# Rows of x1 stored behind the last packed load, x1's turns one chunk ahead and in both halves, first pieces of x0T and Wk at the head of a queue each

## The chip, the cores and the metric

The kernel runs on one core of one Trainium2 chip. The metric is the device time in microseconds (us) of one execution. TensorE (PE) multiplies, VectorE (DVE) and ScalarE (ACT) work on rows of elements, GpSimd (POOL) does the same more slowly, and SyncE (SP) mostly issues DMA transfers. Each engine takes its instructions in the order of the program, and the engines wait for each other by semaphores.

## The reference, cut to what matters

Four layers follow each other on x with 2 x 1024 rows of 512; each one adds its result to its input and normalizes the row.

```
x = layernorm(x + linear_attention(x))       # k = elu(x Wk)+1, q = elu(x Wq)+1, v = x Wv
x = layernorm(x + fp4_swiglu(x))             # weights: 4-bit codes with a scale per group of 128
x = layernorm(x + gated_linear_attention(x)) # 16 chunks of 64 rows per batch
x = layernorm(x + expert_choice_ffn(x))      # the 512 best rows of each batch
```

The second layer is `y = (silu(x Wg) * (x Wu)) Wd` with 1408 inner features, then y over its root mean square. The change touches the first layer's start, the unpacking of the 4-bit weights, and the way the first layer's result x1 gets into the second layer.

## The kernel before

The rows are worked on in four blocks of 512 (`blk` 0 to 3, two per batch).

**First layer, from 0 to about 243 us.** The schedule of this part is made by a scheduler: it keeps an order by priority, readiness and its own estimate of times; `tc.issue_after(x)` and the helper `behind()` (which is `issue_after` of the last PE instruction) hold instructions back behind another. The loads at the top are in pieces so that PE can start early: `part_of_Wk` (L166, on SP) and `part_of_x` (L169, on ACT or SP). Before them PE runs seven products of ones, `idle` (L358). Block 0's k is made by plain products `kp` (L637): for each k of four contraction pieces, four row tiles, with k = 0 cut in two halves of 256 columns. Later projections use `by_seven` (L390), seven products in place of eight, with copies from PE's bank such as L411 and L417. `layernorm` of blocks 0 to 2 is done in `o_products`: statistics on DVE (L226, L227), a power and four normalizing passes on POOL (L221).

**Unpacking.** `unpack` (L281) loads a packed weight piece `pk` (L285, on SP, two buffers), shifts and masks it on DVE (L288, L289) and converts it on ACT (L292). 27 such pieces are spread by `unpack_some` over the first layer. SP issues its DMAs in order, so what stands behind a waiting DMA waits too.

**How x1 gets turned.** Block 0 is transposed on PE. For blocks 1 to 3 the normalized rows are stored to DRAM by `put_rows` (L246) and read back by `get_squares` (L255) in 32 x 32 squares into a tile `x1S`; then `turn_x1` (L1086, DVE) transposes inside the squares a quarter at a time, `high_part` (L1091, ACT) rounds the quarter to a high part and `low_part` (L1095, DVE) subtracts to get the low part. `turn_x1` of a quarter comes before its two parts.

**Second layer, from about 243 to 490 us.** This loop is in an order written out by hand (`manual_schedule`), for PE, ACT, DVE and POOL. A chunk is 128 of the 1408 inner features for one block: 11 chunks a block, n from 0 to 43. In each half of step n:

```python
old.step(0, 2 + half, ACT)      # gate of chunk n-1, contraction piece 2 or 3
new.step(0, half, ACT)          # gate of chunk n, piece 0 or 1
old.step(1, 2 + half, DVE)      # up of chunk n-1
new.step(1, half, ACT)          # up of chunk n
y_pair(m, part)                 # two row tiles of the down product of an earlier chunk
for job in later.get((n, half), ()):
    job()
```

`step` is a product on PE (`in_two`, L950, high and low part), followed by a scaling of the bank in place by ACT (L975) or DVE (L977); the last piece of a gate gives the silu on ACT (L979), the last piece of an up gives `whole` on DVE (L981), which POOL splits (L983, L984). The next piece is added into the scaled bank, so PE needs each scaling. `y_pair` multiplies each down product by a ratio on DVE (L1009). The jobs in `later`, filled by `add(n, half, job)`, are appended to the end of a half: the turns and parts of x1, the statistics (L226) and the scaling (L1023) of the block before, stores and loads, turns of x2.

Of the kernel before, what the change touches and what calls it, by code (L numbers as in the profile page):

```python
# [24 lines left out]
KC = C // P  # L25
I_FF = 1408
NI = I_FF // P
# [46 lines left out]
def body(ctx: ExitStack, tc: tile.TileContext, a: dict, out: bass.AP):  # L74
    nc = tc.nc
# [12 lines left out]
    def bank(ring, name):  # L88
        i = rings[ring][turn_of[ring] % len(rings[ring])]
        turn_of[ring] += 1  # L90
        return psum.tile([P, 512], F32, tag=f"bank{i}", name=name)
# [15 lines left out]
    def wgu_at(k, at, n):  # L107

        i = sum(at >= to for to in gu_parts[1:])
        return wgu[i][:, k, at - gu_parts[i] : at - gu_parts[i] + n]  # L110
# [35 lines left out]
    def xT_slot(i, name, dtype=F32):  # L146
        return xtp.tile([P, KC, 512], dtype, tag=f"xT{i}", name=name)

    def new_xT(blk):
        t = xT_slot(blk % 2, f"x0T{blk}")  # L150
        return t, a["xT"][:, blk * 512 : (blk + 1) * 512].rearrange("(k p) t -> p k t", p=P)
# [12 lines left out]
    t, src = new_xT(0)  # L164

    def part_of_Wk(k, at, to):  # L166
        nc.sync.dma_start(out=Wk[:, k, at:to], in_=a["WkT"][k * P : (k + 1) * P, at:to])

    def part_of_x(by, k, at, to):  # L169
        by.dma_start(out=t[:, k, at:to], in_=src[:, k, at:to])  # L170

    part_of_Wk(0, 0, 256)
    part_of_x(nc.scalar, 0, 0, 128)
    part_of_x(nc.sync, 0, 128, 512)
    for k in range(1, KC):
        part_of_x(nc.scalar, k, 0, 512)
    part_of_Wk(0, 256, 512)
    for k in range(1, KC):
        part_of_Wk(k, 0, 512)
    xT = {0: t}  # L180
# [60 lines left out]
    def put_rows(blk, name, part=range(4)):  # L241

        if (blk, name) not in rows_of:
            rows_of[blk, name] = dram.tile([512, C], F32, name=f"{name}{blk}")
        at, to = part[0], part[-1] + 1
        nc.sync.dma_start(  # L246
            out=rows_of[blk, name][P * at : P * to].rearrange("(c p) d -> p c d", p=P), in_=x_t[blk][:, at:to]
        )

    def get_squares(blk, name, room, part=range(4)):  # L250

        at, to = part[0], part[-1] + 1
        src = rows_of[blk, name][P * at : P * to].rearrange("(tr j) (k g i) -> g j k tr i", j=32, k=KC, g=4)
        for g in range(4):
            nc.sync.dma_start(out=room[32 * g : 32 * g + 32].rearrange("j k (tr i) -> j k tr i", i=32), in_=src[g])  # L255
# [25 lines left out]
    def unpack(parts_, packed, n):  # L281

        pk = dq.tile([P, 704], I32, tag="pk", name="pk")[:, :n]
        src = bass.AP(packed.tensor, packed.offset, [packed.ap[0], (0, 8), packed.ap[1]])
        nc.sync.dma_start(out=pk, in_=src)  # L285


        nc.vector.tensor_scalar(pk, pk, shift, 3, ALU.logical_shift_left, ALU.arith_shift_right)  # L288
        nc.vector.tensor_scalar(pk, pk, CODE, None, ALU.bitwise_and)  # L289
        half = pk.bitcast(F16).rearrange("p (n two) -> p n two", two=2)[:, :, 1]  # L290
        for dst, cut in parts_:
            nc.scalar.activation(dst, half[:, cut], AF.Copy, scale=UNIT)  # L292

    def unpacking():
        n = 704
        for at in range(0, 2 * I_FF, n):
            borders = [at, *(x for x in gu_parts if at < x < at + n), at + n]
            for g in range(KC):
                yield [
                    (wgu_at(g, i, j - i), slice(i - at, j - at)) for i, j in zip(borders, borders[1:])  # L300
                ], a["gu"][16 * g : 16 * (g + 1), at : at + n], n
        for g in (*range(3, NI), *range(3)):
            yield [(wdn_group(g), slice(0, C))], a["dn"][16 * g : 16 * (g + 1), :], C

    to_unpack = unpacking()
    last_elu = [None]
    anchor = [None]

# [45 lines left out]
    nc.vector.memset(ones, 1.0)  # L354

    idle = bank("acc", "idle")
    for _ in range(7):
        ins = nc.tensor.matmul(idle[:, :P], ones, ones, start=True, stop=True).ins  # L358
    last_pe = [ins]

    def behind():

        return ExitStack() if last_pe[0] is None else tc.issue_after(last_pe[0])
# [188 lines left out]
    def o_products(blk):  # L552

        A11, A12, A21, A22 = (qT[blk][:, 2 * e : 2 * e + 2, 256 * t : 256 * t + 256] for t in range(2) for e in range(2))
        G = G_of[blk // 2]
        B11, _, B21, B22 = (G[:, 2 * e : 2 * e + 2, 256 * o : 256 * o + 256] for e in range(2) for o in range(2))
        T1, T2, T3, T4 = TG[blk // 2]

        def product(ps, a, b, first, t, o):

            with behind():
                for r in range(2):
                    for k in range(2):
                        ins = nc.tensor.matmul(
                            ps[:, 256 * r : 256 * r + 256], a[:, k, r * P : (r + 1) * P], b[:, k],
                            start=first and r == 0 and k == 0, stop=k == 1, skip_group_check=True,
                        ).ins
            last_pe[0] = ins
            x = x_t[blk][:, 2 * t : 2 * t + 2, 256 * o : 256 * o + 256]
            return nc.vector.tensor_add(x, x, ps.rearrange("p (r c) -> p r c", r=2)).ins  # L570

        if blk not in S_of:
            q_sums(blk)
        S1, S2 = S_of[blk]
        grow = acc_bank("grow")
        added = product(grow, A11, B11, True, 0, 0)
        with tc.issue_after(added):
            for rest in TG_rest:
                rest()
            TG_rest.clear()  # L580
            nc.vector.tensor_sub(A21, A11, A21)
        yield
        product(acc_bank("P2"), A12, B21, True, 0, 0)
        yield
        product(grow, S2, T2, False, 1, 0)
        nc.vector.tensor_sub(A12, A12, S2)
        yield
        side = acc_bank("P7")
        product(side, A21, T3, True, 1, 1)
        yield  # L590
        product(grow, S1, T1, False, 1, 1)
        yield
        product(side, A22, T4, False, 1, 0)
        yield
        product(grow, A12, B22, False, 0, 1)
        yield
        mv = mv_of[blk] = sp.tile([P, 4, 2], F32, tag="mv", name="mv")
        with tc.issue_after(weighed[0]):
            for i in range(4):
                row_stats(mv[:, i], x_t[blk][:, i])  # L600
            layernorm(x_t[blk], mv, by=nc.gpsimd)
        if blk:
            put_rows(blk, "x1r")
        yield

    def add_o(blk, i):
# [23 lines left out]
    pairs_of["k", 0] = [new_pair(f"k{t}") for t in range(2)]  # L630
    rings["mm"] = (4, 5, 1, 3)
    first = [mm_bank("kp") for _ in range(4)]
    with behind():
        for k in range(KC):
            for i in range(4):
                for o in (slice(0, 256), slice(256, 512)) if k == 0 else (slice(0, 512),):
                    ins = nc.tensor.matmul(  # L637
                        first[i][:, o], xT[0][:, k, tile_of(i)], Wk[:, k, o],
                        start=k == 0 and o.start == 0, stop=k == KC - 1, skip_group_check=True,
                    ).ins  # L640
    last_pe[0] = ins
    rings.update(mm=(0, 1), sum=(2, 3))
    turn_of.update(mm=0)
    Ts = {"k": sums_of_weights(Wk, slices(Tk, 0, 3))}
# [48 lines left out]
    for b in range(B):  # L693
        i, j = 2 * b, 2 * b + 1
# [42 lines left out]
        more()  # L737
    late = mv_of[3]
    unpack_some(1000)
    squares = {1: xT_slot(0, "x1S")}  # L740
    get_squares(1, "x1r", squares[1])
    sg = wk.tile([KC * FG, P], F32, name="sg", bufs=1)
    nc.gpsimd.tensor_copy(sg, gus)
    pg = mm_bank("pg")
# [186 lines left out]
    with tc.tile_pool(name="s2", bufs=1) as wk2:  # L931
# [144 lines left out]
        def add(n, half, job):  # L1076
            later.setdefault((n, half), []).append(job)
# [6 lines left out]
        def turn_x1(blk, i):  # L1084
            x1T[blk, i] = square_tile("x1T")
            nc.vector.transpose(x1T[blk, i], squares[blk][:, :, tile_of(i)])  # L1086

        def high_part(blk, i):
            if i == 0:
                parts_of[blk] = split_tiles(blk)  # L1090
            nc.scalar.copy(parts_of[blk][0][:, :, tile_of(i)], x1T[blk, i])  # L1091

        def low_part(blk, i):
            hi, lo = (t[:, :, tile_of(i)] for t in parts_of[blk])
            nc.vector.tensor_sub(lo, x1T[blk, i], hi.bitcast(F32))  # L1095
# [12 lines left out]
            nc.vector.transpose(xT[blk][:, :, tile_of(i)], squares[blk, i])  # L1108

        for blk in range(1, NB):  # L1110
            first = 5 if blk == 1 else NI * blk - 5
            for i in range(4):
                add(first + i, 1, lambda blk=blk, i=i: turn_x1(blk, i))
                add(first + i + 1, 0, lambda blk=blk, i=i: high_part(blk, i))
                add(first + i + 1, 1, lambda blk=blk, i=i: low_part(blk, i))
        add(8, 0, lambda: put_rows(3, "x1r"))
        add(NI + 1, 0, lambda: get_x1(2))
        add(2 * NI + 1, 0, lambda: get_x1(3))
        for blk in range(2):
            first = (23, 34)[blk]  # L1120
# [833 lines left out]
    _, xs = fetch(0)  # L1954
# [88 lines left out]
```

## Time and profile before

| | |
|---|---|
| median of 3 runs | 912.48 us (911.91 to 913.32) |
| profiled execution, its own time | 912.31 us |
| its span, first to last instruction | 910.5 us |
| busy: PE, DVE, ACT, POOL | 98%, 76%, 42%, 29% of the span |
| mean granted clock of PE | 0.997 |
| DMA | 60.66 MB, mean 67 GB/s |

The span is what the views below divide; the time of the execution is 1.8 us longer. PE's busy time says where PE had a product in flight, not that it ran at its best pace, so the waits and the pace of its products are read beside it. A number in square brackets in the timeline is the engine's idle time before an instruction and what ended it. An engine name with a q (SPq) is the queue that issues DMAs.

### The profile page before, as it was taken

What the parts mean: (1) busy time and instruction counts of PE and PEld (TensorE: products, weight loads), DVE (VectorE), ACT (ScalarE), POOL (GpSimd) and SP (SyncE); (2) the same over time, 40 slices, a digit from 0 to 9 for tenths busy, and PEclk for the clock granted to TensorE, in tenths of its full rate; (3) what the DMA queues carried; (4) which work ended last, traced back from release to release, by engine and by line L of the source; (5) the groups of instructions that cost most, each with busy time, mean ns of one, the idle gap of its engine ahead of it and who ended that gap; (6) DMA issues with size and microseconds to landing.
All of it is one profiled execution on the core that took longest, in us unless ns stands there. A gap on an engine that the chain in (4) does not pass through costs nothing.

```text
span 910.5 us, 10938 instructions
## 1 busy us (share of the span) xinstructions
PE 888.3 (98%) x3955; PEld 692.6 (76%) x3955; DVE 693.7 (76%) x1324; ACT 378.6 (42%) x644; POOL 263.4 (29%) x229
## 2 busy tenths in 40 slices
PE   8999999999999999999999999999999999999996
PEld 5667885688577887877877677788676888888886
DVE  2558994588879789798879875857977886898535
ACT  1345341454467786876867534131201223120000
POOL 0120074200474357457564302020250030000112
PEclk9999999999999999999999999999999999999999
DMA  9532222200441402604201500000024220230001
GB/s 328 195 112 67 74 75 81 68 14 1 86 135 46 47 1 56 84 1 114 72 0 47 208 1 1 1 1 1 0 93 139 94 85 9 99 133 1 13 35 47
DMA packets 70391, 60.66 MB, mean 67 GB/s; under 512 B 46622, under 2 KB 47178, under 8 KB 69825
## 3 DMA queue, kind: packets, MB, share of 16 engines
q1 hardware_dynamic: 67841, 54.89, 20.7%
q0 software_dynamic: 1920, 4.22, 1.2%
q10 hardware_dynamic: 576, 0.85, 0.3%
q8 instruction: 31, 0.51, 0.2%
q14 instruction: 23, 0.19, 0.1%
HBM read 46.27 MB, written 15.78 MB: 68 GB/s over the span
## 4 chain that ended last, share of the span: by engine, by line
PE 78%; DVE 13%; POOL 3%; issue 2%; ACT 2%; DMA 1%; POOLq 0%; SPq 0%; DVEq 0%; ACTq 0%
PE yp L1726 10%; PE hp L1640 9%; PE yp L950 8%; PE upp L950 8%; PE gatep L950 8%; PE go L918 7%; PE xk L441 5%; PE grow L390 4%; PE P L390 3%; PE kp L637 2%; PE ao L611 2%; PE ao L1513 2%; PE grow L1479 1%; DVE cmp L1564 1%; PE op L1351 1%
## 5 line engine op out<-in xcount | busy, mean ns | idle before, releaser
L1009 DVE TENSOR_TENSOR yp<-yp,ratio 128x512 f32<-128x512 f32 x160 | 103.2, 691 | 10.3 <-PE yp L950 9.9
L219 POOL TENSOR_TENSOR rs<-rs,table 128x4 f32<-128x4 f32 (+1 forms) x19 | 17.2, 904 | 293.9 <-DVE rs L218 293.7
L975 ACT ACTIVATE gatep<-gatep,scale 128x512 f32<-128x512 f32 x132 | 83.8, 656 | 40.0 <-PE gatep L950 37.2
L950 PE MATMUL gatep<-x1Tl,wgu 128*128 128x512 f32 x176 | 69.5, 395 | 3.5 <-DVE x1Tl L1095 3.2
L950 PE MATMUL upp<-x1Th,wgu 128*128 128x512 f32 x176 | 69.8, 396 | 0.7 <-DVE upp L977 0.7
L950 PE MATMUL gatep<-x1Th,wgu 128*128 128x512 f32 x176 | 70.3, 399 | 0.0
L950 PE MATMUL yp<-wdn,hlo 128*128 128x512 f32 x176 | 69.9, 397 | 0.2 <-POOL hlo L984 0.2
L950 PE MATMUL yp<-wdn,hhi 128*128 128x512 f32 x176 | 69.9, 397 | 0.0
L950 PE MATMUL upp<-x1Tl,wgu 128*128 128x512 f32 x176 | 68.9, 391 | 0.0
L975 ACT ACTIVATE upp<-upp,scale 128x512 f32<-128x512 f32 x88 | 57.8, 662 | 9.6 <-PE upp L950 3.6
L984 POOL TENSOR_TENSOR hlo<-whole,hhi 128x512 fp32r<-128x512 f32 x43 | 56.2, 1306 | 3.5
L983 POOL CAST hhi<-whole 128x512 fp32r<-128x512 f32 x43 | 26.3, 611 | 91.7 <-DVE whole L981 90.6
L981 DVE SCALAR_TENSOR_TENSOR whole<-upp,scale,silu 128x512 f32<-128x512 f32 x43 | 32.1, 747 | 19.7 <-PE upp L950 13.3
L918 PE MATMUL go<-spare,spare 128*128 128x256 f32 x192 | 44.0, 381 | 0.0
L441 PE MATMUL xk<-pair,x 128*128 128x512 f32 x96 | 42.7, 592 | 0.0
L226 DVE BATCH_NORM_STATS2 st<-x 128x6 f32<-128x512 f32 x64 | 42.3, 675 | 0.4
L950 PEld LDWEIGHTS gatep<-x1Tl,wgu 128*128 128x128 f32 x176 | 33.1, 188 | 12.1 <-DVE x1Tl L1095 4.1
L950 PEld LDWEIGHTS upp<-x1Th,wgu 128*128 128x128 f32 x176 | 33.0, 188 | 10.0 <-DVE upp L977 2.8
L1373 POOL TENSOR_TENSOR sum<-sum,sq 128x512 f32<-128x512 f32 x12 | 18.2, 1520 | 77.1 <-issue 67.5
L918 PEld LDWEIGHTS go<-spare,spare 128*128 128x128 f32 x192 | 36.0, 190 | 5.8 <-issue 1.2
L950 PEld LDWEIGHTS yp<-wdn,hhi 128*128 128x128 f32 x176 | 33.0, 188 | 9.5 <-DVE yp L1009 1.1
L950 PEld LDWEIGHTS gatep<-x1Th,wgu 128*128 128x128 f32 x176 | 33.1, 188 | 9.0 <-ACT gatep L975 1.1
(472 smaller groups left out, 2108.9 us busy)
## 6 DMA issues: line engine op xcount, KB each, us to landing
pk<-in_gu SPq DMA_DIRECT2D x16, 352.0 KB, 3.7
x<-in_x SPq DMA_DIRECT2D x4, 1024.0 KB, 15.3
w<-in_w SPq DMA_DIRECT2D x1, 4096.0 KB, 13.5
xs<-picked SPq DMA_DIRECT2D x4, 1024.0 KB, 5.1
out<-x SPq DMA_DIRECT2D x4, 1024.0 KB, 4.7
w<-in_w SPq DMA_DIRECT2D x4, 1024.0 KB, 5.5
x0T<-in_xT SPq DMA_DIRECT2D x3, 1024.0 KB, 6.9
x1r<-x SPq DMA_DIRECT2D x3, 1024.0 KB, 5.1
```

Source lines behind the costliest of these rows:

```text
L226: nc.vector.bn_stats(st, x)
L390: ins = nc.tensor.matmul(ps[:, 256 * r : 256 * r + 256], a[:, k, r * P : (r + 1) * P], b[:, k], start=first and r == 0 and k == 0, stop=k ...
L441: ins = nc.tensor.matmul(acc_of[b][c], x_t[blk][:, i, c * P : (c + 1) * P], pairs_of["k", blk][i // 2][:, i % 2], start=blk % 2 == 0 and i ...
L918: ins = nc.tensor.matmul(ps[:, 256 * m : 256 * m + 256], w[:, k, m], b[:, k, 256 * half : 256 * half + 256], start=first and m == 0 and k ...
L950: nc.tensor.matmul(ps, w, x, start=start and n == 0, stop=stop and n == 1, skip_group_check=True)
L975: nc.scalar.activation(ps, ps, AF.Copy, scale=s)
L981: nc.vector.scalar_tensor_tensor(self.whole, ps, s, self.silu, ALU.mult, ALU.mult)
L983: nc.gpsimd.tensor_copy(hi, self.whole)
L984: nc.gpsimd.tensor_sub(lo, self.whole, hi.bitcast(F32))
L1009: nc.vector.tensor_tensor(self.y[:, i] if g == NI - 1 else ps, ps, ratio[:, g], ALU.mult)
L1640: ins = nc.tensor.matmul(ps[:, 256 * j : 256 * j + 256], pair_of(w, g)[:, k, j], x[:, k], start=k == 0, stop=k == 1).ins
L1726: nc.tensor.matmul(ps[:, 256 * r : 256 * r + 256], x(r, j), w(j), start=j == 0, stop=j == NJ - 1)
```

## The change

Five things are changed; every other instruction stays, though some move.

1. The first pieces of x0T (columns 0 to 128, then 128 to 512) are both issued by ACT, the first pieces of Wk (columns 0 to 256, then 256 to 512) both by SP. Before, SP issued Wk's first piece, then x0T's second, then Wk's second.
2. Nine instead of seven products of ones. The `kp` products are held in the order written; before, only the group as a whole was held behind the products of ones, and the scheduler had put one that needs x0T's second piece first.
3. `put_rows` for blocks 1 and 2 no longer stands in `o_products`, but after all unpacking, behind the last packed load `last_pk`, with the reads back of block 1.
4. The first quarter's turn is at step 6, first half, for block 1 (before: step 5, second half), and at step 11 blk - 6, first half, for blocks 2 and 3 (before: 11 blk - 5, second half).
5. The high part is in the same half as its turn, and the low part in the second half of that step. Before, the turn was in a second half and both parts in the step after it, in its first and second half. So all of blocks 2 and 3 is split two steps earlier than before; block 1's parts stay where they were, and its turns come half a step later.

In the order of the built programs, PE's instructions differ only by the two products of ones. On DVE and ACT a few instructions of the first layer change places (around 44 us two packed pieces' shifts; around 145 us ACT converts a third packed piece ahead of the copy L411). On SP the store of block 1 goes from between two packed loads to behind the last one, directly ahead of the reads back; the store of block 2 keeps its place between two of these reads; the loads and stores of x2's rows interleave differently.

```diff
-    part_of_Wk(0, 0, 256)
-    part_of_x(nc.scalar, 0, 0, 128)
-    part_of_x(nc.sync, 0, 128, 512)
+    for at, to in ((0, 128), (128, 512)):
+        part_of_x(nc.scalar, 0, at, to)
+    for at in (0, 256):
+        part_of_Wk(0, at, at + 256)
     for k in range(1, KC):
         part_of_x(nc.scalar, k, 0, 512)
-    part_of_Wk(0, 256, 512)
     for k in range(1, KC):
         part_of_Wk(k, 0, 512)
...
-        nc.sync.dma_start(out=pk, in_=src)
+        last_pk[0] = nc.sync.dma_start(out=pk, in_=src).ins
...
-    for _ in range(7):
+    for _ in range(9):
         ins = nc.tensor.matmul(idle[:, :P], ones, ones, start=True, stop=True).ins
...
             layernorm(x_t[blk], mv, by=nc.gpsimd)
-        if blk:
-            put_rows(blk, "x1r")
         yield
...
-    with behind():
-        for k in range(KC):
-            for i in range(4):
-                for o in (slice(0, 256), slice(256, 512)) if k == 0 else (slice(0, 512),):
-                    ins = nc.tensor.matmul(
+    for k in range(KC):
+        for i in range(4):
+            for o in (slice(0, 256), slice(256, 512)) if k == 0 else (slice(0, 512),):
+                with behind():
+                    last_pe[0] = nc.tensor.matmul(
                         first[i][:, o], xT[0][:, k, tile_of(i)], Wk[:, k, o],
                         start=k == 0 and o.start == 0, stop=k == KC - 1, skip_group_check=True,
                     ).ins
-    last_pe[0] = ins
...
-    squares = {1: xT_slot(0, "x1S")}
-    get_squares(1, "x1r", squares[1])
+    with tc.issue_after(last_pk[0]):
+        put_rows(1, "x1r")
+        put_rows(2, "x1r")
+        squares = {1: xT_slot(0, "x1S")}
+        get_squares(1, "x1r", squares[1])
...
-            first = 5 if blk == 1 else NI * blk - 5
+            first = 6 if blk == 1 else NI * blk - 6
             for i in range(4):
-                add(first + i, 1, lambda blk=blk, i=i: turn_x1(blk, i))
-                add(first + i + 1, 0, lambda blk=blk, i=i: high_part(blk, i))
-                add(first + i + 1, 1, lambda blk=blk, i=i: low_part(blk, i))
+                add(first + i, 0, lambda blk=blk, i=i: turn_x1(blk, i))
+                add(first + i, 0, lambda blk=blk, i=i: high_part(blk, i))
+                add(first + i, 1, lambda blk=blk, i=i: low_part(blk, i))
```

The changed program has one source line more, so from line 306 on its line numbers differ by one from those of the kernel before.

More of the change, by code (lines that the diff above doesn't have):

```diff
@@ L305, in body @@
     to_unpack = unpacking()
+    last_pk = [None]
     last_elu = [None]
```

## Prediction

> **What bounds the kernel now.** I read the page's busy shares first (PE 98%), then who PE waited for, because with PE this full a change can only win in a PE wait or lose by making one. Columns: total us, times, longest.
>
> ```profile
> PE gatep L950 <- DVE x1Tl L1095: 3.2, 2, 1.6
> PE grow L390 <- ACT pair L417: 2.2, 1, 2.2
> ...
> PE kp L637 <- DMA x0T<-in_xT: 1.3, 1, 1.3
> ```
>
> All three lie where the change works; together 6.7 us. Then the timeline around the second wait, and the windows there (seventh value: granted clock).
>
> ```profile
> 157.59 0.49 DVE L288 TENSOR_SCALAR pk<-pk,shift 128x512 int32<-128x512 int32 x1 [12.33 <-DMA pk<-in_dn]
> ...
> 159.59 0.57 ACT L417 COPY pair<-grow 128x512 f32<-128x512 f32 x1
> 160.21 3.68 PE L390 MATMUL grow<-Wk,rw 128*128 128x256 f32 x8 [2.22 <-ACT pair L417]
> ```
>
> ```profile
> 160.00:164.00 4.00, 3.79 (x10) 3.06 (x11) 2.28 (x5) 1.53 (x4) 0.00 (x0) 0.57 0.19 66
> ```
>
> DVE stood 12.33 us for a packed load. ACT's unpack of it stands ahead of L417, which frees PE's bank. The eight passes of L390 then took 3.68 us where others take 1.89, at half clock. Why the load was late is in SP's own waits:
>
> ```profile
> SPq L246 <- POOL x L221: 13.6, 1, 13.6
> ```
>
> The store of block 1's x1 waits for POOL's norm with the packed loads queued behind it.
>
> Last, the SwiGLU loop. A chunk where nothing else intrudes runs at PE's pace: L981 starts at 323.42 and 328.97, 5.55 us. Here are a half chunk of it, and the same place in a chunk with turns (L1086) and copies (L1091):
>
> ```profile
> 326.94 1.30 DVE L1009 TENSOR_TENSOR yp<-yp,ratio 128x512 f32<-128x512 f32 x2 [0.16 <-PE yp L950]
> ...
> 327.88 0.69 ACT L979 ACTIVATE silu<-gatep,scale 128x512 f32<-128x512 f32 x1
> ...
> 328.46 0.65 ACT L975 ACTIVATE gatep<-gatep,scale 128x512 f32<-128x512 f32 x1
> ...
> 330.00 0.40 PE L950 MATMUL gatep<-x1Th,wgu 128*128 128x512 f32 x1
> ```
>
> ```profile
> 280.49 1.48 DVE L1095 TENSOR_TENSOR x1Tl<-x1T,x1Th 128x512 fp32r<-128x512 f32 x1
> ...
> 281.89 0.70 DVE L1086 STREAM_TRANSPOSE x1T<-x1S 128x512 f32<-128x512 f32 x1
> ...
> 282.52 0.71 DVE L977 TENSOR_SCALAR upp<-upp,scale 128x512 f32<-128x512 f32 x1
> ...
> 282.62 0.62 ACT L1091 CAST x1Th<-x1T 128x512 fp32r<-128x512 f32 x1 [0.37 <-DVE x1T L1086]
> ...
> 283.15 1.28 DVE L1009 TENSOR_TENSOR yp<-yp,ratio 128x512 f32<-128x512 f32 x2
> 283.15 0.68 ACT L979 ACTIVATE silu<-gatep,scale 128x512 f32<-128x512 f32 x1
> ```
>
> The reader is to see the order on ACT: the copy L1091 stands directly ahead of the silu L979, and waits for the turn on DVE. Today the turn is the last job of the half before, so the copy waits 0.37 us at most here.
>
> **Part 1, the first loads.** Today the first product in PE's order needs x0T's columns 128 to 512, second on SP; PE idles 1.30 us, later 0.24 for Wk's second piece, and runs at half clock to 10.1 us: the first 512-wide pass starts at 11.71. In the changed kernel the first product needs only the piece at the head of each queue (64 KB, landed after 2.7 us; 128 KB, after 2.5 us, so at 3.4 and 3.2). Nine warm-up products make 18 passes of 0.21 us, ending at 4.9. The sixteen 256-wide passes then need 16 x 0.216 = 3.5 us at full clock, to 8.3: 3.4 us saved. That assumes full clock by 4.9. The trace's half-clock record lasted 3.41 us, so unbroken work from 1.04 should be at full clock after one to two such stretches, between 4.5 and 7.9; the later end costs half of 3.0 us, leaving 1.9 saved. I take 2.8, between the ends. Hidden: the pieces for k = 1. They need 1 MB in by 8.3; today about as much had moved by 7.4, and the last of Wk's second piece landed before 8.0. If they land as late as today (DVE gets Wk's at 9.43), 2.3 is saved. What is released by loads until 35 us (scales for the down weights, at 36.6 on DVE today) then has up to 1 us less room; no PE work hangs on it before 50 us. All later work is released by PE, so I carry the 2.8 through.
>
> [...]
>
> **Part 2, the stores behind the packed loads.** The L246 of block 1 leaves the middle of the loads. The next packed load then waits only for its buffer, which ACT frees at 145.2 (L292, 144.55 + 0.68); earlier loads here landed 3.1 to 3.3 us after issue, so at 148.5 instead of 157.5. In the new order ACT's L411 stands behind that unpack: DVE 148.5 to 149.5, ACT to 150.2, L411 to 150.8. PE needs its bank at 152.67, 1.9 us later; that is the cover. Then L417 is done by 155.2 and PE goes on at 157.8 instead of 160.21 (2.4) and at full clock (8 x 0.21 = 1.7): 4.1 us saved. From below: 2.4, if the clock drops elsewhere. The moved store, about 5.1 us, goes out near 180 on an idle SP, with the reads back of block 1 behind it; those wait until 227 for their buffer, so it is hidden. The store of block 2 keeps its place between the reads.
>
> [...] The half clock came after a PE wait of 2.22 us. [...]
>
> **Part 3, the turns.** Each of the twelve quarters of blocks 1 to 3 now has turn and high copy in the same first half, in this order: DVE L977, L1009, L1009, turn; ACT upp, copy, silu. So silu waits for copy, copy for turn, turn for both L1009, and L981, next on DVE, waits for silu.
> - First quarter of a block, on the chunk shown: L1009 ends at 328.24, turn at 328.85, copy starts 328.89, silu (0.52 later) 329.41 instead of 327.88: 1.53 late. The cover is what the scaled gate (328.46 + 0.65 = 329.11) has before PE reads it at 330.00, 0.83 with 0.06 of hand-over. PE stalls 0.7. In blocks 2 and 3 an L1023 (0.61) lies between copy and silu: 1.3.
> - Next quarters: after silu DVE has a closed loop. Start to start: L981 0.65, four L1009 2.40, L1095 1.40 (the usual length beside POOL's L984), L977 0.63, turn 0.70, hand-over 0.04, copy 0.52, silu 0.69, hand-over 0.04: 7.07 us a chunk, 1.5 over PE's 5.55. PE's work fits inside the loop, so its time follows it.
> - In blocks 2 and 3 one statistics pair (0.79) lies in the loop of the second and third chunk: 2.3 each. The other pair falls into DVE's wait for silu.
>
> After: block 1 0.7 + 3 x 1.5 = 5.2; blocks 2 and 3 each 1.3 + 2.3 + 2.3 + 1.55 = 7.45; sum 20.1. Before, by starts of L981 against 5.55 a chunk: 0.4 over chunks 6 to 10, 2.6 to chunk 22, 2.55 to chunk 33; sum 5.55, the two 1.6 us waits for L1095 among them. Those waits go, since the last low part comes two chunks earlier. Net 14.6 lost. From below: if every L1095 in the loop ran at its shortest (0.77), nine times 0.68 less, 8.5. From above: 0.1 more hand-over in each of nine loops and 0.1 more on L1095, 16.4.
>
> **Sum.** Span 910.5, the execution's own time 912.31 (0.2 below the median 912.48): 912.3 - 2.8 - 4.1 + 14.6 = 920.0.
>
> **Rivals.**
> - Faster: the silu's delay is covered. That needs copy and silu to be less than 0.83 us late in the twelve chunks; then only the gains stay: 912.3 - 2.8 - 4.1 - 3.2 = 902.2. For: PE waited only 0.7 us for L977 in this loop with DVE full. Against: the turn ends 0.7 us after silu's usual start even with DVE idle before. Chance 0.11.
> - Short low parts: 912.3 - 6.9 + 8.5 = 913.9. For: two of today's twelve took 0.77. Against: the other ten took about 1.4. Chance 0.07.
> - The store's wait turns into one for L411 behind three unpacks, decided if a packed load takes 1.9 us longer than 3.3, as one beside the store did (5.7): no 4.1, so 924.1. Chance 0.06.
> - PE's stalls drop its clock: nine loops with up to 1.7 us more, some 8 us in all, 928. Against: the 1.60 us wait at 360.89 left the clock at 1.00. Chance 0.04.
>
> **How the numbers follow.** The forecast has the remaining 0.72, with 920.0 and its own range from the bounds 1.9 to 3.4, 2.4 to 4.1, and 12.5 to 16.4 (three of the nine low parts short at best): 917 to 924. The overall range reaches down to the short low parts, 913.5, and up to 925; the covered case, the clock case and the edges are left out. A run of this kernel can tell 0.2%, 1.8 us, from no change. Faster by more: 0.11. Within: 0.04, the lower half of the short low parts. Slower: 0.85.
>
> **What would show it.** Right: in the changed profile ACT's L1091 waits for the turn by over 1 us in each of twelve chunks, DVE's L981 waits for silu, PE's first gate product after each waits on ACT, and L981 starts 7 us apart; no half-clock record near 160 and no wait at L417; the first 512-wide pass near 9. Wrong: turns lying in idle DVE time with PE unbroken through chunks 6 to 9, or a new wait of PE before 165 us.

## The result, and the profile after

The changed kernel takes 921.4 us (median of 4 runs, 920.74 to 921.91) where the kernel before took 912.3 on the same chip (911.91 to 913.32): ratio 1.0098, interval 1.0080 to 1.0115. The profiled execution took 921.91 us, its span is 920.1. In the second layer its line numbers are one higher than before: the copy of the high part is L1092, the low part L1096, the silu L980, `whole` L982, the products L951.

PE's waits in the changed kernel (total us, times, longest):

```profile
PE gatep L951 <- ACT gatep L976: 15.6, 12, 1.5
PE upp L951 <- DVE upp L978: 1.5, 4, 0.4
```

The three waits shown of before are gone. In their place stands the first line: twelve waits, one for each quarter of blocks 1 to 3, for ACT's scaling of a gate. (Before, the second line stood at 0.7 us in two waits.) Who makes ACT late is in ACT's waits from 255 to 436 us:

```profile
ACT x1Th L1092 <- DVE x1T L1087: 31.3, 12, 3.3
```

ACT stands idle ahead of the copy of the high part until its turn is done, 2.6 us on average and never under 1.75 (0.37 in the chunk shown of before). Not all of that is lost, since ACT has slack; the timeline of one chunk shows what is.

```profile
272.95 0.70 DVE L1087 STREAM_TRANSPOSE x1T<-x1S 128x512 f32<-128x512 f32 x1
...
273.69 0.62 ACT L1092 CAST x1Th<-x1T 128x512 fp32r<-128x512 f32 x1 [2.54 <-DVE x1T L1087]
...
274.21 0.68 ACT L980 ACTIVATE silu<-gatep,scale 128x512 f32<-128x512 f32 x1
...
274.98 0.75 DVE L982 SCALAR_TENSOR_TENSOR whole<-upp,scale,silu 128x512 f32<-128x512 f32 x1 [1.33 <-issue]
...
275.50 0.50 PE L951 MATMUL gatep<-x1Th,wgu 128*128 128x512 f32 x1 [1.34 <-ACT gatep L976]
```

Turn, copy, silu, the scaled gate, PE: each starts as the one before it ends, and DVE waits at L982 for the silu too. (This row names no releaser, but the silu ends at 274.89; six of DVE's other waits at L982, 6.0 us in all, are put down to it.) In this block L982 starts at 267.82, 274.98, 282.14 and 289.29, 7.16 us apart, where PE alone needs 5.55.

The place of the packed loads, in DVE's and PE's timelines and in the window 160 to 164 us (the seventh value is the granted clock, 0.57 before):

```profile
146.47 0.49 DVE L288 TENSOR_SCALAR pk<-pk,shift 128x512 int32<-128x512 int32 x1 [3.29 <-DMA pk<-in_dn]
```

```profile
152.30 3.60 PE L442 MATMUL xk<-pair,x 128*128 128x512 f32 x8
155.74 1.89 PE L391 MATMUL grow<-Wk,rw 128*128 128x256 f32 x8
```

```profile
160.00:164.00 4.00, 4.00 (x17) 2.95 (x17) 2.30 (x5) 1.96 (x4) 3.12 (x3) 1.00 0.00 1
```

DVE waits 3.29 us for the packed load in place of 12.33, no wait stands ahead of PE's eight passes, and they take 1.89 us, not 3.68.

The start, in PE's timeline:

```profile
1.04 4.21 PE L359 MATMUL idle<-ones 128*128 128x128 f32 x18 [1.04 <-DVE ones L355]
5.30 10.90 PE L636 MATMUL kp<-Wk,x0T 128*128 128x256 f32 x31
```

The products follow the warm-up without a gap; the first 512-wide pass starts at 9.61 instead of 11.71.

Laying PE's products of the two traces side by side, each against the same product before, gives where the 9.6 us between the spans come from: -2.1 by the 512-wide passes, another -4.15 by 164 us, and +15.85 in the second layer. (The expectations below take 3.95 and 15.7 for the last two.)

### The profile page after: what moved, and what is told of

It is laid out like the page before. It is cut to its first block, busy times and chain, and to the rows that moved or that the text cites. A ratio compares the mean times of both kernels' runs of the same rounds, so it can differ in the third digit from the quotient of the medians.

```text
span 920.1 us, 10946 instructions
## 1 busy us (share of the span) xinstructions
PE 888.3 (97%) x3959; PEld 691.0 (75%) x3959; DVE 697.8 (76%) x1324; ACT 377.3 (41%) x644; POOL 263.4 (29%) x229
## 4 chain that ended last, share of the span: by engine, by line
PE 44%; DVE 7%; issue 1%; ACT 1%; POOL 0%; POOLq 0%
PE yp L1727 10%; PE hp L1641 9%; PE go L919 7%; PE yp L951 3%; PE gatep L951 3%; PE upp L951 3%; PE ao L1514 1%; PE grow L1480 1%; DVE cmp L1565 1%; PE op L1352 1%; PE op L1364 1%; DVE cmp L1562 1%; PE P L1480 1%; DVE st L226 1%; DVE cmp L1568 1%
## 5 line engine op out<-in xcount | busy, mean ns | idle before, releaser
L1010 DVE TENSOR_TENSOR yp<-yp,ratio 128x512 f32<-128x512 f32 x160 | 103.2, 692 | 10.5 <-PE yp L951 10.2
L951 PE MATMUL gatep<-x1Th,wgu 128*128 128x512 f32 x176 | 71.5, 406 | 15.6 <-ACT gatep L976 15.6
L951 PE MATMUL upp<-x1Th,wgu 128*128 128x512 f32 x176 | 69.3, 394 | 1.5 <-DVE upp L978 1.5
L951 PE MATMUL yp<-wdn,hhi 128*128 128x512 f32 x176 | 70.1, 398 | 0.0
L951 PE MATMUL yp<-wdn,hlo 128*128 128x512 f32 x176 | 69.8, 397 | 0.2 <-POOL hlo L985 0.2
L951 PE MATMUL gatep<-x1Tl,wgu 128*128 128x512 f32 x176 | 69.3, 394 | 0.3 <-DVE x1Tl L268 0.3
L951 PE MATMUL upp<-x1Tl,wgu 128*128 128x512 f32 x176 | 68.9, 391 | 0.0
L985 POOL TENSOR_TENSOR hlo<-whole,hhi 128x512 fp32r<-128x512 f32 x43 | 55.4, 1289 | 3.5
L984 POOL CAST hhi<-whole 128x512 fp32r<-128x512 f32 x43 | 26.3, 611 | 105.5 <-DVE whole L982 104.1
L982 DVE SCALAR_TENSOR_TENSOR whole<-upp,scale,silu 128x512 f32<-128x512 f32 x43 | 32.3, 751 | 31.8 <-PE upp L951 11.5
L951 PEld LDWEIGHTS gatep<-x1Th,wgu 128*128 128x128 f32 x176 | 33.0, 188 | 29.3 <-ACT gatep L976 21.9
L226 DVE BATCH_NORM_STATS2 st<-x 128x6 f32<-128x512 f32 x64 | 42.3, 677 | 0.4
L951 PEld LDWEIGHTS upp<-x1Th,wgu 128*128 128x128 f32 x176 | 33.0, 188 | 10.5 <-DVE upp L978 3.2
L951 PEld LDWEIGHTS yp<-wdn,hhi 128*128 128x128 f32 x176 | 33.0, 188 | 9.5 <-DVE yp L1010 1.1
L978 DVE TENSOR_SCALAR upp<-upp,scale 128x512 f32<-128x512 f32 x44 | 33.0, 751 | 8.4 <-PE upp L951 7.8
```

Of the source, the lines that this page charges most:

```text
L226: nc.vector.bn_stats(st, x)
L951: nc.tensor.matmul(ps, w, x, start=start and n == 0, stop=stop and n == 1, skip_group_check=True)
L978: nc.vector.tensor_scalar(ps, ps, s, None, ALU.mult)
L982: nc.vector.scalar_tensor_tensor(self.whole, ps, s, self.silu, ALU.mult, ALU.mult)
L984: nc.gpsimd.tensor_copy(hi, self.whole)
L985: nc.gpsimd.tensor_sub(lo, self.whole, hi.bitcast(F32))
```

## The experiments

Theory A: the turns alone lose the time, because the copy stands ahead of the silu on ACT and waits for the turn. Theory B: DVE has too much work in these chunks, wherever it stands. Times are medians; "before" is the kernel before on the same chip. The runs were made on three chips, whose "before" lies between 911.91 and 912.62, so a difference between rows of two chips is sure only to some 0.7 us. The line numbers in diffs and profiles are those of each kernel.

| kernel | us | before | ratio, 95% interval |
|---|---|---|---|
| turns alone (part 3) | 928.45 | 912.04 | 1.0178, 1.0164 to 1.0192 |
| no turns (parts 1 and 2) | 905.57 | 912.04 | 0.9927, 0.9914 to 0.9941 |
| copy alone later | 906.96 | 912.62 | 0.9945, 0.9928 to 0.9961 |
| late copy and low part | 902.04 | 912.04 | 0.9888, 0.9873 to 0.9903 |
| turn half a chunk earlier | 907.88 | 912.04 | 0.9954, 0.9940 to 0.9967 |
| the same, low part later | 901.95 | 912.62 | 0.9891, 0.9871 to 0.9911 |
| low part alone later | 917.74 | 911.91 | 1.0064, 1.0051 to 1.0077 |
| first loads alone (part 1) | 909.23 | 911.91 | 0.9965, 0.9952 to 0.9977 |
| stores alone (part 2) | 907.95 | 911.91 | 0.9955, 0.9943 to 0.9967 |
| late copy, seven warm-up products | 902.01 | 911.91 | 0.9889, 0.9875 to 0.9904 |

### The parts by themselves

**Turns alone.** The kernel before with this edit only:

```diff
-            first = 5 if blk == 1 else NI * blk - 5
+            first = 6 if blk == 1 else NI * blk - 6
-                add(first + i, 1, lambda blk=blk, i=i: turn_x1(blk, i))
-                add(first + i + 1, 0, lambda blk=blk, i=i: high_part(blk, i))
-                add(first + i + 1, 1, lambda blk=blk, i=i: low_part(blk, i))
+                add(first + i, 0, lambda blk=blk, i=i: turn_x1(blk, i))
+                add(first + i, 0, lambda blk=blk, i=i: high_part(blk, i))
+                add(first + i, 1, lambda blk=blk, i=i: low_part(blk, i))
```

> The kernel before with the third part alone (turn, copy and low part of each quarter in one chunk, as after). Theory A (the turns alone lose the time, by the silu waiting behind the copy): the loss in the loop as read from the two traces is 15.7 us, so 912.3 + 15.7 = 928.0; the prediction's own sum would give 912.3 + 14.6 = 926.9. Rival, that the early order of x1 (stores moved behind the packed loads) is what spoils the loop: less than 5 us lost, below 917.

Measured: 928.45, 16.4 us more than before. The loss is the turns' own; the early order of the stores has no share in it.

**No turns.** The kernel after with that edit undone.

> The kernel after with the turns where the kernel before has them: parts 1 and 2 alone. If the drifts read from the traces hold by themselves: 912.3 - 2.1 (start) - 3.95 (stall and half clock near 160 us) = 906.2, and the two PE waits for the low part at the ends of blocks come back (1.6 us each). Rival, that a gain at the start is given back later in the front part because what is released by loads has less room: 908 to 910.

Measured: 905.57, 6.5 us less than before; nothing is given back later. Its span is 903.9, 16.2 less than after's. PE's products are 0.3 us ahead of after's before the second layer is reached (the first 512-wide pass starts at 9.27, not 9.61), so the turns cost 15.9 us. The two waits for the low part at the ends of blocks are back (3.2 us).

### What makes the turns slow

**Copy alone later.** After, with ACT's copy half a chunk later and nothing else moved:

```diff
-                add(first + i, 0, lambda blk=blk, i=i: high_part(blk, i))
+                add(first + i, 1, lambda blk=blk, i=i: high_part(blk, i))
```

> The kernel after with ACT's copy alone half a chunk later: DVE's order is after's, word for word (turn in the first half, low part in the second). Theory A (the copy's place ahead of silu): the waits of PE for the scaled gate vanish and most of the 19.4 us between after (921.4) and the late copy (902.0) comes back, 903 to 908; what is left is the long low part (1.48 us beside POOL's L985), as in the run with the turn half a chunk earlier (907.9). Theory B (DVE's order and its 5.9 us a chunk): 917 to 921. Possible price: the low part now waits for a copy that stands behind the scalings of the same half on ACT, with L978 and L1010 queued behind it on DVE; if that wait is 0.5 us or more in each chunk, 910 or more.

Measured: 906.96. DVE's order is after's, and 14.4 us are back. PE's waits, and ACT's timeline:

```profile
PE upp L951 <- DVE upp L978: 4.4, 4, 1.5
```

```profile
276.61 0.69 ACT L980 ACTIVATE silu<-gatep,scale 128x512 f32<-128x512 f32 x1 [0.73 <-PE gatep L951]
...
278.56 0.61 ACT L1092 CAST x1Th<-x1T 128x512 fp32r<-128x512 f32 x1
```

The silu waits for nothing but its own gate product, the copy for nothing at all, and the twelve waits for the scaled gate are gone. That is theory A. The possible price that was named, a low part waiting for the late copy, does not show. What is left is a wait of another kind, for the scaled up part, on DVE.

**Late copy and low part.** The low part moved along, half a chunk later:

```diff
-                add(first + i, 0, lambda blk=blk, i=i: high_part(blk, i))
-                add(first + i, 1, lambda blk=blk, i=i: low_part(blk, i))
+                add(first + i, 1, lambda blk=blk, i=i: high_part(blk, i))
+                add(first + i + 1, 0, lambda blk=blk, i=i: low_part(blk, i))
```

> The kernel after, the turn where it is (first half of the chunk), the copy half a chunk later and the low part one half later with it. Theory A (ACT's order: the copy ahead of the silu waits for the turn, and everything behind waits with it): the copy finds its turn done half a chunk ago, silu starts on time, PE's waits for the scaled gate vanish, and the loss of 15.7 us against the kernel before with its own turns goes: 904 to 907. Theory B (DVE: turn 0.70 and low part 1.48 in the same chunk as 3.7 us of other DVE work make 5.9 us where PE has 5.55, more with statistics, and where they stand does not matter): the loss stays for the most part, 917 to 921, and L982 starts stay 7 us apart.

Measured: 902.04, 2 us better than the best that theory A named. Neither kind of wait is left (two new ones, for `whole`, make 0.7 us); the low part's group line (durations in ns: shortest, median, longest), in after and then in this kernel, tells why:

```profile
L1096 DVE TENSOR_TENSOR x1Tl<-x1T,x1Th x12: 1479/1484/1492, 269.7 to 423.8; 128x512 fp32r<-128x512 f32 x12
```

```profile
L1096 DVE TENSOR_TENSOR x1Tl<-x1T,x1Th x12: 672/681/745, 271.2 to 407.2; 128x512 fp32r<-128x512 f32 x12
```

The same subtraction takes less than half the time in its new place.

**Turn half a chunk earlier.** After, with the turn as the last job of the half before:

```diff
-                add(first + i, 0, lambda blk=blk, i=i: turn_x1(blk, i))
+                add(first + i - 1, 1, lambda blk=blk, i=i: turn_x1(blk, i))
```

> The kernel after, with only the turn half a chunk earlier, as the last job of the half before; copy and low part stay where after has them. Blocks 2 and 3 are then one chunk ahead of the kernel before. Theory A (copy waits for turn ahead of silu): the copy waits 0.4 us at most, as in the kernel before, no loop through ACT forms, and the two waits for the low part at the ends of blocks are gone since it comes a chunk earlier: 912.3 - 2.1 - 3.95 - 3.2 = 903.0, or up to 906 if other small stalls take the place of those. Theory B (too much DVE work in these chunks): 917 to 921.

Measured: 907.88, beyond what either theory said, though far nearer to A. PE's waits, and a stretch of POOL's and DVE's timelines:

```profile
PE upp L951 <- DVE upp L978: 5.7, 6, 1.5
```

```profile
330.83 1.29 POOL L985 TENSOR_TENSOR hlo<-whole,hhi 128x512 fp32r<-128x512 f32 x1
```

```profile
331.19 1.48 DVE L1096 TENSOR_TENSOR x1Tl<-x1T,x1Th 128x512 fp32r<-128x512 f32 x1
332.59 0.70 DVE L1087 STREAM_TRANSPOSE x1T<-x1S 128x512 f32<-128x512 f32 x1
...
334.00 0.73 DVE L978 TENSOR_SCALAR upp<-upp,scale 128x512 f32<-128x512 f32 x1
```

DVE has no gap here. The low part starts beside POOL's L985 and takes 1.48 us; L978, on which PE waits, stands behind it, with the turn and one statistics pair (L226, L227) between.

**The same, low part later.** To see whether the low part's length is that loss:

```diff
-                add(first + i, 1, lambda blk=blk, i=i: low_part(blk, i))
+                add(first + i + 1, 0, lambda blk=blk, i=i: low_part(blk, i))
```

> The kernel with the turn half a chunk earlier (907.88 us), its low part alone half a chunk later. Theory A2 (what that kernel loses against the late copy is the low part standing beside POOL's L985, which makes it 1.48 instead of 0.68 us while DVE has no time to spare): the low parts take 0.68, PE's waits for the scaled up part (5.7 us in six) go, 902 to 903. Rival (the loss is the turn and the statistics in the same half): 906 to 908.

Measured: 901.95, the low parts 0.68 to 0.75, with the turn and the statistics where they were. The loss hung on the low part's place beside L985: 5.9 us here, 4.9 between the copy alone and the late copy with its low part. How much of it is the longer subtraction and how much the order on DVE was not separated: the six long low parts of blocks 2 and 3 became 4.5 us shorter in all, and the low part also went from ahead of L978 to behind it.

**Low part alone later.** The last edit made to after itself, turn and copy left where after has them.

> The kernel after, turn and copy where it has them, the low part alone half a chunk later, ahead of the next turn. Theory A (a closed loop through DVE, ACT's copy and silu sets the chunk): the low part then stands far behind L982 as it does in the run with the late copy, where it took 0.68 instead of 1.48 us, so the loop shrinks from 7.16 to 6.3 to 6.4 us a chunk (L982 0.66, four L1010 2.40, L978 0.66, low part 0.60, turn 0.63, hand-over 0.04, copy 0.52, silu 0.69, hand-over 0.09); nine loops of about 0.8 less, 921.4 - 7 = 914.5; PE's waits for the scaled gate stay, shorter. Theory B (the copy's place alone costs the time, and the low part lies in slack): no change, 920.5 to 922.

Measured: 917.74. This expectation missed by 3 us: the low parts took 0.68, but the chunk shrank to 6.97 us, not to 6.3. DVE, ACT and PE in one chunk of that kernel:

```profile
276.21 0.76 DVE L978 TENSOR_SCALAR upp<-upp,scale 128x512 f32<-128x512 f32 x1 [0.26 <-PE upp L951]
...
277.13 1.30 DVE L1010 TENSOR_TENSOR yp<-yp,ratio 128x512 f32<-128x512 f32 x2 [0.16 <-PE yp L951]
...
278.33 0.68 DVE L1096 TENSOR_TENSOR x1Tl<-x1T,x1Th 128x512 fp32r<-128x512 f32 x1
...
278.93 0.70 DVE L1087 STREAM_TRANSPOSE x1T<-x1S 128x512 f32<-128x512 f32 x1
...
279.67 0.62 ACT L1092 CAST x1Th<-x1T 128x512 fp32r<-128x512 f32 x1 [2.35 <-DVE x1T L1087]
...
280.20 0.68 ACT L980 ACTIVATE silu<-gatep,scale 128x512 f32<-128x512 f32 x1
...
280.78 0.65 ACT L976 ACTIVATE gatep<-gatep,scale 128x512 f32<-128x512 f32 x1
...
281.48 0.50 PE L951 MATMUL gatep<-x1Th,wgu 128*128 128x512 f32 x1 [1.14 <-ACT gatep L976]
```

DVE now waits for PE at L978 and L1010: a second loop has taken over. It leads from the stalled gate product at 274.51 over the up product to L978 (1.70 us later), the first L1010 (0.92), the low part (1.20), the turn (0.60), the copy (0.74), the silu (0.53), the gate's scaling (0.58) and back to PE (0.70): 6.97 us. In after the low part is not in that loop: it starts at 276.84, ahead of L978 (278.26), and in DVE's timeline of after the turn follows directly on the two L1010:

```profile
278.92 1.28 DVE L1010 TENSOR_TENSOR yp<-yp,ratio 128x512 f32<-128x512 f32 x2
280.12 0.69 DVE L1087 STREAM_TRANSPOSE x1T<-x1S 128x512 f32<-128x512 f32 x1
```

There the first L1010 starts 3.42 us after the stalled product at 275.50, where PE needs only the 2.62 of this kernel; an estimate for the loop through PE in after is 6.97 - 0.60 = 6.37. So the edit took 0.8 out of DVE's own loop of 7.16 and put 0.60 into the other one, which then set the pace: 0.19 gained. In the steps with statistics, where DVE's loop was 7.95, the chunk fell to 7.14.

### The first loads and the stores

**First loads alone.** The kernel before with the first hunk of the change, the nine warm-up products and the `kp` products held one behind the other.

> The kernel before with part 1 alone (order of the first loads, nine warm-up products, the 256-wide products recorded one behind the other). Theory A (the start is 2.1 to 2.4 us shorter, as the drift between the traces says): 912.1 - 2.2 = 909.9. Rival C (most of that is where the half rate of the first products happens to end: the profiled run of the kernel with the turns alone had the old loads and yet was 2.0 us ahead of the kernel before after its first 24 products): no more than the 1.3 us of the removed wait for x0T, 910.8 to 912.

Measured: 909.23, 2.7 us less than before (2.1 to 4.4 by the interval): theory A, a little more than it said.

**Stores alone.** The kernel before with `last_pk` and the two `put_rows` behind it.

> The kernel before with part 2 alone (rows of block 1 and 2 stored behind the last packed load). Theory A: the wait of 2.22 us and the half clock behind it both go, 912.1 - 3.95 = 908.1. Rival C (the half clock does not follow the wait in every run; in the profiled run of the turns alone the wait of 2.2 us stood and the products behind it ran at full rate): 912.1 - 2.4 = 909.7, or between the two.

Measured: 907.95, 4.0 us less than before: theory A. Rival C is not idle, though. In two other kernels the wait that this part removes was still there. PE's timeline of the turns alone, then of the first loads alone, and the latter's window from 159 to 160 us:

```profile
158.02 1.99 PE L390 MATMUL grow<-Wk,rw 128*128 128x256 f32 x8 [2.17 <-ACT pair L417]
```

```profile
157.29 2.94 PE L390 MATMUL grow<-Wk,rw 128*128 128x256 f32 x8 [2.16 <-ACT pair L417]
```

```profile
159.00:160.00 1.00, 1.00 (x3) 0.75 (x3) 0.62 (x2) 0.35 (x1) 0.00 (x0) 0.50 0.00 0
```

Behind the same wait of 2.2 us, PE ran at full clock in one profile (1.00 from 158 to 163 us), at half clock from 0.9 us after the wait in the other (0.59 from 158 to 159, 0.50 to 161), and at half clock from 0.1 us after it in the kernel before. So 4.0 (3.0 to 5.2 by the interval) is what this part is worth in the median of several runs; in the single run it is between 2.2, the wait, and about 4.

**Seven warm-up products** in the kernel of the late copy:

```diff
-    for _ in range(9):
+    for _ in range(7):
```

> The kernel of the late copy (902.04 us) with seven warm-up products instead of nine. The first pieces lie in SBUF from 3.4 us, the eighteen passes end at 5.2. With fourteen the products could begin at 4.3. If the first four 256-wide passes alone can start early (the rest of x0T landed at 5.8): up to 0.9 us less, 901.2. Rival: PE then waits for x0T at about 5.2, a gap that puts off the full rate of the products: same or up to 1 us more, 902 to 903.

Measured: 902.01, no change. The first product starts at 4.45 instead of 5.31, but the first 512-wide pass at 9.18 instead of 9.40: the clock is full from 6.84 instead of 6.43 us, and what was begun earlier ran at half rate. The rival's outcome came with another cause; no wait for x0T is listed.

## Why the prediction was right

**Turns, +14.6 forecast.** The order on ACT was read right, and each sign that was named is there: twelve copies waiting over 1 us, L982 behind the silu, PE waiting on the gate in each of the twelve chunks, starts about 7 us apart. The term was 1.3 us short of the 15.9. By PE's gate products the first step of block 1 cost 0.72 us, that of blocks 2 and 3 1.33 each, as forecast (0.7 and 1.3). Each loop took 0.1 more than the sum, 7.16 us for 7.07 and 7.95 for 7.86 with statistics, 0.9 in nine loops; the step behind each block's last loop cost another 0.1, which the sum left out. No entry of the loop was far off: start to start, the low part took 1.42 for 1.40, L978 0.66 for 0.63, silu to L982 0.77 for 0.73.

The rival of short low parts (913.9) stays untested: in after's place all twelve stood beside L985 and took 1.48 to 1.49, and the run that had them all short, at 917.7, had them in the second loop. Its price mixes lengths with times from start to start: 1.40 is a time from start to start, while 0.77 is a length, and the ten long ones of before took 1.39 to 1.49. The cover of the silu (0.83 us against a delay of 1.53) decided the sign as worked out: PE's first loss was the 0.7 between them. The rival of the covered silu did not come about; the copy half a chunk later ends the silu's wait, but that alone gave 907.0. Only with the low part moved too is the time 902.0, where the prediction had put that case at 902.2.

**Stores, -4.1 forecast.** -4.15 between the traces, -4.0 alone. L411 kept its cover, and no wait took the place of the old one. The prediction took one row, half clock behind a wait of 2.22 us, for what such a wait costs. The row was not the whole story: three profiles gave three outcomes for one wait, so the 1.7 us of half clock in the term did not come with every wait of this length, and that the term came out so close is in part luck. The half-clock record near 160 us lasts 3.413 us in the kernel before (the windows of the first loads alone give 3.4 too). The three stretches at full clock between two changes in the traces of before and after last 150.186, 744.106 and 907.945 us, 44.0, 218.0 and 266.0 times that.

Count steps of 3.413 us back from the fall to half clock. In the kernel before the wait (157.99 to 160.21) lies whole in one step, 156.90 to 160.31, and half clock follows at 160.31; in the first loads alone (155.13 to 157.29) it lies whole in the step 154.78 to 158.19, and half clock follows at 158.19. In the turns alone the wait (155.85 to 158.02) left the clock at 1.00, with no fall to count from, so whether the place of a wait in such a step decides was not shown. The wait of 1.60 us that ends at 360.89 in the kernel before and those of up to 1.47 us in after's loops left the clock full.

**First loads, -2.8 forecast.** -2.1 between the two traces, -2.7 alone. "Between 4.5 and 7.9" was right for the end of the half clock: with the new loads it came at 6.85 us in after, and at 6.43 and 6.84 in the late copy with nine and with seven warm-up products; the first 512-wide pass began at 9.61, 9.40 and 9.18, and at 9.27 without the turns (8.91 forecast). The nine warm-up products ended at 5.25 and not at 4.9: 18 times 0.21 is too little, since the 14 passes of before already took 3.36. With the old loads it began at 11.71 in the kernel before, 9.56 in the turns alone and 12.07 in the stores alone, so the difference of two single profiles could have shown anything from 0 to 2.9; only repeated runs size this part. x0T's second piece landed at 5.80 us, at 5.56 in the kernel before: no sooner for its new queue. But PE, still at half clock, reached the first product that needs it only at 6.7, so it was the clock and not the load that set the start.

## What to carry to other kernels

An instruction that waits for another engine belongs on an in-order engine behind the work that the critical engine needs next, not ahead of it: here half a chunk on ACT was worth 14.4 us, and with the low part moved too the kernel beats both, at 902.0 us (ratio 0.9888 to before). When a loop through several engines sets the pace and an instruction is moved out of it, price also the loop that it is moved into; and do not size a part that hangs on the clock from one pair of profiles.

## What the runs showed of the hardware

Where a low part on DVE and POOL's subtraction (L984 in before, L985 in after) met in these two traces, the one that started later took longer: a low part 1.39 to 1.49 us, against 0.68 in the late copy, and POOL's 1.61 against 1.29. In the kernel before, POOL and DVE in one chunk, and then in a later one where DVE came first:

```profile
342.06 1.29 POOL L984 TENSOR_TENSOR hlo<-whole,hhi 128x512 fp32r<-128x512 f32 x1
342.42 1.48 DVE L1095 TENSOR_TENSOR x1Tl<-x1T,x1Th 128x512 fp32r<-128x512 f32 x1
```

```profile
348.20 0.77 DVE L1095 TENSOR_TENSOR x1Tl<-x1T,x1Th 128x512 fp32r<-128x512 f32 x1
...
348.51 1.61 POOL L984 TENSOR_TENSOR hlo<-whole,hhi 128x512 fp32r<-128x512 f32 x1
```

In the first, POOL ends at 343.36 and the low part 0.55 us behind it; in after each of the twelve low parts ends 0.54 to 0.55 us behind the end of L985. In the second, DVE keeps nearly its 0.68 us and POOL's 1.29 become 1.61. POOL's L1058 (one operand and scalars) showed this in one order only. In the late copy's kernel a low part that started at 339.92, 0.56 us into an L1058 of 2.08, took 0.74 us, so it was hardly held. But the three L1058 that started 0.92 to 0.93 us into a low part of after took 2.51 us, where eleven of its sixteen there take 2.07 to 2.08.

How much time is spent at half clock differs from run to run of one kernel: the turns alone, with the old loads and the old wait, ran once in 925.28 us with a mean clock of 0.998 and four times in 927.66 to 928.86 with 0.994 or 0.995. A difference of 0.004 over 927 us is 3.7 us of clock, about the spread of the times (3.6).
